# A graph-attention kernel that multiplies by seven products: accumulators in pairs of PSUM banks, emptied by one operation

## The chip, the cores and the metric

The kernel runs on one core of one Trainium2 chip. The metric is the device time of one execution in microseconds (us), the median of several runs. Besides, one execution was recorded by the hardware profiler; its span is counted from the first to the last instruction of the program.

In what follows PE is the matrix engine, PEld its weight load, DVE the vector engine, ACT the scalar engine, POOL the GpSimd engine and SP the engine that issues most DMAs.

## The reference

For each of 32 batch elements x is a 512x512 matrix and adj a 512x512 matrix of zeros and ones. Two graph-attention layers follow each other, the first with four heads of 256 columns, the second with one head of 512:

```python
def gat_layer(x, mask, W, a_src, a_dst, bias, concat):
    xl = (x @ W).reshape(B, N, H, F)
    asrc = jnp.einsum('bnhf,hf->bnh', xl, a_src)
    adst = jnp.einsum('bnhf,hf->bnh', xl, a_dst)
    e = jax.nn.leaky_relu(asrc[:, :, None, :] + adst[:, None, :, :], NEG_SLOPE)
    e = jnp.where(mask[..., None], e, NEG_INF)
    attn = jax.nn.softmax(e, axis=1)
    out = jnp.einsum('bsdh,bshf->bdhf', attn, xl)
    ...
    return out + bias

h = jnp.maximum(_layernorm(x, axis=-1), 0.0)
h = jax.nn.elu(gat_layer(h, mask, W1, att_src1, att_dst1, b1, concat=True))
h = gat_layer(h, mask, W2, att_src2, att_dst2, b2, concat=False)
return x + h
```

All of it is in fp32. Since the softmax sums to one over the sources, adding b2 to each row of the second layer's xl gives the same output as adding b2 to the output.

## The kernel before, in words

Every large product is a 2x2 block product computed with seven block products instead of eight (numbered 1 to 7 in the code). Each of them is a handful of matmuls of a 128x128 stationary block with 256 to 258 moving columns that accumulate in a PSUM bank. The four output blocks are sums of the seven products. Part of these sums is made in PSUM: products 1, 6, 7 and 4 go one after another onto one bank (called a in the code), 5 and 3 onto a second (b), and 2 has a third (g). After each product the bank's present content is read, and the product of the next number accumulates on top of it. So a product on bank a must wait until the content before it has been read.

There are four such stages in a batch element b:

- project1 (line 905): h @ W1, in four units (two row halves of 128 for two pairs of heads), two weight blocks a product, 258 columns (256 and two score columns);
- gather1 (line 1008): attention times xl in layer 1, two units at a time, which are two heads, 256 columns;
- project2 (line 1068): @ W2, two units, four weight blocks a product, 257 columns;
- gather2 (line 1143): attention times xl2 in layer 2, two units, 256 columns.

The matmuls of three of them are laid by `sevens` (line 813), those of gather1 by its own loop. Both take a list that gives the order of (unit, product): TWO, LAST, FOUR, PARTS (lines 840 to 850), PAIRS_OF and, for the last batch element, SINGLY (lines 999 and 1002). For example LAST runs (0,1), (1,1), (0,5), (1,5), (0,6), (1,6), (0,3), (1,3), (0,7), (1,7), (0,2), (1,2), (0,4), (1,4). A bank is one of eight tiles of 512 fp32 columns (line 358), handed out in turn.

What happens after a product is in `put` (line 804) and in gather1: products 1, 4, 5 and 6 are copied by ACT to where the output block lies in SBUF, and 2, 3 and 7 are added to it by DVE:

```python
if n in (1, 4, 5, 6):
    act(COPY, [bk], keys, d, ps, AF.Copy, scale=-1.0)
else:
    dve(ADD, [bk] + keys, keys, nc.vector.tensor_sub, d, d, ps)
```

In gather2 DVE adds each of the seven to a tile that holds x, and there `residual` (line 1103) has loaded x for four row blocks of 128 into four t tiles and has added the bias b2 to each with one DVE operation of 128x512 (line 1114). The t tiles (line 348) serve also as room for the sums t1 and t2 of the right operand in `sums1` (line 956), two for each head. `sums1` makes, for one head, four sums of xl blocks (128x256) and three or four of attention blocks (128x512).

The order of the work is not the order in which the loop at line 1258 states it. Each operation is put on record with its engine, a cost in us, what it reads and writes (lines 378 to 399), and a planner (class Program) lays out the order of each engine. PE's order is that of the program. For ACT, DVE, POOL and SP it takes among the operations that are ready the one with the most urgent rank, and it tries many ranks against its own account of costs. The result is a fixed order for each engine, kept by semaphores at run time. In the program's order the main loop runs gather1 of heads 0 and 1, the first half of project1 of the next batch element, gather1 of heads 2 and 3, the second half of project1, gather2, and project2 of the next element.

In the profile all matmuls bear line 396, all ACT operations line 379, all DVE operations line 382 and most DMAs line 385, as they are issued by helpers. Groups are told apart by tiles: xl<-mm is a copy or sum of project1 or project2, h<-mm or h<-h,mm one of gather1, t<-mm,t one of gather2, t<-t,b_sb the bias.

Of the kernel before, what the change touches and what calls it, by code (L numbers as in the profile page):

```python
# [10 lines left out]
F32 = mybir.dt.float32  # L11
# [19 lines left out]
class Slots:  # L31
# [9 lines left out]
    def give(self, key):  # L41
        self.free.append(key[1])

# [213 lines left out]
def tile_gat(  # L257
# [76 lines left out]
    b2_sb = sbuf.tile([P, DO], F32, name="b2_sb")  # L334
# [8 lines left out]
    adjs = slots("adj", 2, [P, N], I32)  # L343
# [4 lines left out]
    ts_ = slots("t", 4, [P, N])  # L348
# [9 lines left out]
    banks = slots("mm", 8, [P, 512], F32, psum)  # L358
# [42 lines left out]
    COPY, ADD, TINY = 0.28, 0.34, 0.1  # L401

# [54 lines left out]
    def weights2():  # L457

        for (r, c), ix in AT.items():
            dma(  # L460
                1.5, [("ht", 0, 0)], [("w2", ix)], w2_sb[:, ix, :, 1 - c : W2H - c],
# [6 lines left out]
        dma(0.75, (), ["b2"], b2_sb, rows_of(b2, P))  # L468
        for a, v in enumerate((as2, ad2)):
            lk, bc = ts_.take()  # L470
            dma(0.75, (), [lk], bc, rows_of(v[0], P))
            for (r, c), ix in AT.items():
                for k in range(KH):
# [4 lines left out]
                        junk[:, : DO // 2], w2_sb[:, ix, k, 1 - c : W2H - c], 1.0,  # L478
# [5 lines left out]
        for a in range(2):  # L484
            for r in range(2):
                g = part[:, a, r * KH : (r + 1) * KH, :]
                col = slice(0, 1) if a == 0 else slice(W2H - 1, W2H)
# [3 lines left out]
                    w2_sb[:, AT[r, a], :, col], g[:, :, 0:1], g[:, :, 1:2],  # L491
# [308 lines left out]
    def minus(to):  # L800

        def put(n, u, bk, ps):
            d, keys = to(u, *BLOCK[n - 1])
            if n in (1, 4, 5, 6):
                act(COPY, [bk], keys, d, ps, AF.Copy, scale=-1.0)
            else:
                dve(ADD, [bk] + keys, keys, nc.vector.tensor_sub, d, d, ps)

        return put

    def sevens(left, right, rkeys, put, kh, units, width, order):


        bank = {}
        for u, n in order:
            m = units[u][0]
            acc, first = {1: "a", 2: "g", 5: "b", 6: "a", 7: "a", 3: "b", 4: "a"}[n], n in (1, 2, 5)
            if first:  # L820
                bank[u, acc] = banks.take()
            bk, bt = bank[u, acc]
            ps = bt[:, :width]
            a, akeys = left[n]
            pe(
                akeys + rkeys(n), [bk], kh * width / 593,
                [
                    (mm, (ps, a[:, k, m * P : (m + 1) * P], right(n, units[u], k)),
                     dict(start=(first and k == 0), stop=(k == kh - 1), skip_group_check=True))
                    for k in range(kh)  # L830
# [3 lines left out]
            if n in (2, 3, 4):  # L834
                banks.give(bk)
# [517 lines left out]
```

## Time and profile before

| What | us |
|---|---|
| median of 3 runs (lowest to highest) | 2783.35 (2781.97 to 2785.19) |
| span of the profiled execution | 2778.8 |
| DVE, 128x512 bias add, one | 0.689 |
| DVE, 128x258 add from a bank (xl<-xl,mm), one | 0.421 |
| ACT, 128x258 copy from a bank (xl<-mm), one | 0.386 |
| ACT, 128x512 copy from a bank (ht<-mm, eight in the set-up), one | 0.592 |

The profiled execution's span is 4.55 us below the median of the runs; what lies around the span (start and end of the program) is in the run's time and not in the span. A busy share is the time in which at least one instruction of that engine is under way. Matmuls overlap: one takes 0.38 us, and the next begins 0.216 us after it. The durations of ACT and DVE operations overlap at their edges too, so that 372 operations of 0.42 us add up to 149 us of busy time and not to 155.

### The profile page before, as it was taken

Reading aid. Unit: us, or ns where it says so; the run is one execution under the profiler, and the core shown is the slowest. Engines: PE = TensorE matmul, PEld = TensorE weight load, DVE = VectorE, ACT = ScalarE, POOL = GpSimd, SP = SyncE. Lnnn points to the kernel's source line nnn. Section 1 sums busy time; section 2 is a strip of 40 time slices with the busy share of each in tenths; the row PEclk is TensorE's granted clock in tenths of the full one; section 3 lists DMA queues with packets and bytes.
Section 4 is the critical chain, followed back from the end, with each engine's and each line's share of the span. In section 5 each row is a group of like instructions: output and inputs, shape, how many; then the busy total and the mean of one; then the engine's idle time right before and its main releaser. Section 6 shows DMA issues by size and latency. Waiting matters only on the chain. (4 is left out here: it accounts for less than half of the span.)

```text
span 2778.8 us, 41571 instructions
## 1 busy us (share of the span) xinstructions
PE 2746.2 (99%) x12520; PEld 2373.9 (85%) x12520; DVE 2645.4 (95%) x6726; ACT 2304.3 (83%) x4870; POOL 324.7 (12%) x356
## 2 busy tenths in 40 slices
PE   7999999999999999999999999999999999999999
PEld 6688888888888888888888888888888888888887
DVE  7999999999999999999999999999999999998997
ACT  5988888889888888888888888888888888887883
POOL 0110111001111101111011101011110111101110
PEclk9999999999999999999999999999999999999999
DMA  7766767667777667676677766777666867678663
GB/s 228 171 176 178 201 174 199 171 175 181 191 194 174 179 165 203 177 186 184 172 192 184 196 168 175 178 189 195 183 175 175 202 166 202 157 189 182 169 158 107
DMA packets 370964, 501.55 MB, mean 180 GB/s; under 512 B 222260, under 2 KB 226868, under 8 KB 370740
## 3 DMA queue, kind: packets, MB, share of 16 engines
q1 hardware_dynamic: 324948, 332.16, 43.6%
q0 software_dynamic: 45792, 166.74, 25.2%
q8 instruction: 100, 1.64, 0.2%
q14 instruction: 124, 1.02, 0.1%
HBM read 315.89 MB, written 51.31 MB: 132 GB/s over the span
## 5 line engine op out<-in xcount | busy, mean ns | idle before, releaser
L396 PE MATMUL mm<-w_sb,hs 128*128 128x257 f32 (+2 forms) x3032 | 688.5, 381 | 4.9 <-DVE hs L382 2.5
L396 PEld LDWEIGHTS mm<-w_sb,hs 128*128 128x128 f32 x3032 | 575.8, 190 | 92.0 <-ACT xl L379 4.6
L390 POOL DMA_DIRECT2D p<-dm x314 | 276.2, 887 | 2346.3 <-DVE p L382 1600.3
L379 ACT ACTIVATE l<-as,z 128x512 f32<-128x512 f32 x640 | 442.8, 721 | 101.9 <-DMA as<-das 96.2
L379 ACT ACTIVATE l<-l,low 128x512 f32<-128x512 f32 x640 | 459.2, 721 | 49.1 <-DVE low L382 46.0
L396 PE MATMUL mm<-w_sb,ht 128*128 128x258 f32 x2112 | 481.4, 382 | 1.9 <-DVE xl L382 1.4
L396 PE MATMUL mm<-p,xl 128*128 128x256 f32 (+1 forms) x1984 | 468.0, 384 | 1.0 <-DVE h L382 0.8
L396 PE MATMUL mm<-w_sb,h 128*128 128x257 f32 x2056 | 467.8, 379 | 0.0
L379 ACT ACTIVATE p<-p,z 128x512 f32<-128x512 f32 (+1 forms) x636 | 427.2, 716 | 42.6 <-DMA p<-dm 28.1
L382 DVE SCALAR_TENSOR_TENSOR p<-rr,z 128x512 f32<-128x512 f32 (+1 forms) x636 | 449.0, 743 | 11.8 <-DMA rr<-drr 11.6
L396 PEld LDWEIGHTS mm<-w_sb,ht 128*128 128x128 f32 x2112 | 400.9, 190 | 61.8 <-DVE xl L382 4.1
L382 DVE CUSTOM_DVE_ANT_1 l<-l,mt 128x512 f32<-128x512 f32 x640 | 429.1, 685 | 12.0 <-ACT l L379 9.5
L396 PEld LDWEIGHTS mm<-w_sb,h 128*128 128x128 f32 x2056 | 389.4, 189 | 57.8 <-issue 0.5
L396 PEld LDWEIGHTS mm<-p,xl 128*128 128x128 f32 x1984 | 377.1, 190 | 61.7 <-issue 5.7
L379 ACT ACTIVATE xl<-mm 128x258 f32<-128x258 f32 (+2 forms) x748 | 279.8, 382 | 70.6 <-PE mm L396 68.7
L379 ACT ACTIVATE h<-mm 128x256 f32<-128x256 f32 x496 | 181.7, 378 | 91.0 <-PE mm L396 88.4
L382 DVE TENSOR_TENSOR xl<-xl,mm 128x258 f32<-128x258 f32 x558 | 222.8, 420 | 29.1 <-PE mm L396 24.3
L379 ACT ACTIVATE xr<-h,b_sb 128x512 f32<-128x512 f32 x248 | 176.7, 721 | 75.7 <-DVE h L382 72.0
L396 PE MATMUL mm<-t,hs 128*128 128x256 f32 x992 | 226.0, 380 | 2.9 <-ACT h L379 2.9
L396 PEld LDWEIGHTS mm<-t,hs 128*128 128x128 f32 x992 | 188.4, 190 | 29.9 <-ACT h L379 4.7
L382 DVE SCALAR_TENSOR_TENSOR h<-h,b_sb,xr 128x512 f32<-128x512 f32 x248 | 182.9, 747 | 3.2 <-ACT xr L379 3.1
L382 DVE TENSOR_TENSOR t<-mm,t 128x256 f32<-128x256 f32 (+1 forms) x424 | 172.8, 419 | 11.7 <-PE mm L396 10.5
(114 smaller groups left out, 3421.8 us busy)
## 6 DMA issues: line engine op xcount, KB each, us to landing
p<-dm POOLq DMA_DIRECT2D x314, 512.0 KB, 5.2
rr<-drr SPq DMA_DIRECT2D x159, 512.0 KB
x<-in_x_dram SPq DMA_DIRECT2D x129, 256.0 KB
adj<-in_adj_dram SPq DMA_DIRECT2D x128, 256.0 KB
as<-das SPq DMA_DIRECT2D x64, 512.0 KB
t<-in_x_dram SPq DMA_DIRECT2D x124, 256.0 KB
out_dram<-t SPq DMA_DIRECT2D x124, 256.0 KB
dm<-m SPq DMA_DIRECT2D x32, 512.0 KB
```

Of the source, the lines that this page charges most:

```text
L379: prog.add("ACT", cost, reads, writes, lambda: nc.scalar.activation(*a, **k))
L382: prog.add("DVE", cost, reads, writes, lambda: f(*a, **k))
L390: lambda: nc.gpsimd.dma_start(to, at, accum_op=OP.add), size,
L396: f(*a, **k)
```

## The change

The eight single banks become four tiles of two banks each, handed out by a new class. `take2` gives a whole pair, `take` one half. For each bank it keeps how many columns have been written by matmuls since the last fresh start, and a bank that is to be filled by ACT and then accumulated upon is chosen only where that width is enough. Among the fitting pairs the least written is taken.

```diff
+    def able(self, seeded):
+        return any(
+            all(q in self.free and self.written[q] >= seeded for q in ((i, 0), (i, 1)))
+            for i in range(len(self.tiles))
+        )
+    def take2(self, width, seeded=0):
+        whole = [i for i, j in self.free if j == 0 and (i, 1) in self.free]
+        least = {i: min(self.written[i, j] for j in range(2)) for i in whole}
+        i = min((i for i in whole if least[i] >= seeded), key=least.get)
...
+        return [("mm", i, j) for j in range(2)], self.tiles[i]
-    ts_ = slots("t", 4, [P, N])
+    ts_ = slots("t", 2, [P, 2, N])
-    banks = slots("mm", 8, [P, 512], F32, psum)
+    banks = Banks(tiles("mm", 4, [P, 2, 512], F32, psum))
+    COPY2, ADD2 = 0.5, 0.61
```

In `sevens` two units form one step: both products go into the two banks of a pair, and one ACT or DVE operation of twice the width empties both. After product 1 the pair is copied by ACT into a second pair, g, if one is free, and not to the output; product 2 then accumulates on that copy, and g is copied to the output by ACT. So DVE adds product 2 only where there was no pair for the copy. Two of the order lists fall away, and a seed can be laid into a fresh pair before its first product:

```diff
+            acc, first = ACC[n], n in (1, 5) or n == 2 and us not in forked
             if first:
+                seed = seeds.get(n)
+                bank[us, acc] = banks.take2(width, 0 if seed is None else M)
+                if seed is not None:
+                    first = False
+                    bks, bt = bank[us, acc]
+                    act(
+                        COPY2, [seed[1]], bks, bt[:, :, :width],
+                        seed[0][:, None, :].to_broadcast([P, 2, width]), AF.Copy,
+                    )
...
+            if n == 1 and banks.able(width):
+                bank[us, "g"] = gks, gt = banks.take2(width, width)
+                act(COPY2, bks, gks, gt[:, :, :width], bt[:, :, :width], AF.Copy)
+                forked.add(us)
+            else:
+                fresh = n in (1, 4, 5, 6) or n == 2 and us in forked
+                put(n, [units[u] for u in us], bks, bt[:, :, :width], fresh)
...
+    LAST = tuple(((0, 1), n) for n in (1, 5, 6, 3, 7, 2, 4))
+    FOUR = LAST + tuple(((2, 3), n) for _, n in LAST)
+    PARTS = tuple(((0, 1), n) for n in (1, 2, 5, 6, 3, 7, 4))
```

gather1 does the same with two heads as a step (in SINGLY one head, one bank), with the copy of product 1 always made. Its `sums1` makes the four sums of xl for both heads in one operation each, and takes one paired t tile a head, given back when products 5 and 6 are both through:

```diff
-        tuple((h + i, n) for n in (1, 2, 6, 5, 7, 3, 4) for i in range(2)) for h in (0, 2)
+    PAIRS_OF = tuple(tuple(((h, h + 1), n) for n in (1, 5, 6, 2, 7, 3, 4)) for h in (0, 2))
...
-            if n in (1, 4, 5, 6):
-                act(COPY, [bk], [key], to, ps, AF.Copy)
+            if n == 1:
+                bank[u, "g"] = gks, gt = some(len(u), M)
+                act(COPY2 if two else COPY, bks, gks, gt[:, :, :M], ps, AF.Copy)
+            elif n in (2, 4, 5, 6):
+                act(COPY2 if two else COPY, bks, keys, to, ps, AF.Copy)
             else:
-                dve(ADD, [bk, key], [key], nc.vector.tensor_add, to, to, ps)
+                dve(ADD2 if two else ADD, bks + keys, keys, nc.vector.tensor_add, to, to, ps)
```

The bias b2 no longer goes onto x. project2 lays it, with its sign turned, into the pairs of products 1 and 5, and so into the rows of xl2; for this the set-up holds b2 as two halves, the second less the first. Each half of xl2 and of W2 now has its 256 columns first and the score column last. `residual` loads two row blocks with one DMA and adds nothing, and gather2 writes two row blocks out with one:

```diff
+            {1: (b2_sb[:, 0], "b2"), 5: (b2_sb[:, 1], "b2")},
...
-            dma(0.75, [x2_key(b, 0, 0)], halves, xr, x[b, d * P : (d + 1) * P, :])
-            dve(0.59, [xk, "b2"], halves, nc.vector.tensor_add, xr, xr, b2_sb)
+            dma(
+                1.5, [x2_key(b, 0, 0)], halves, xr,
+                x[b, r * 2 * P : (r + 1) * 2 * P, :].rearrange("(m p) f -> p m f", p=P),
+            )
```

Costs and orders that the planner sees change with this, so the orders of ACT, DVE, POOL and SP are laid anew over the whole kernel.

## The prediction

> **What bounds the kernel now.** I read the page's first part, then the windows by stage, then the timeline of PE, then the waits of PE, and last the groups by form for the instructions that the change replaces.
>
> ```profile
> span 2778.8 us, 41571 instructions
> PE 2746.2 (99%) x12520; PEld 2373.9 (85%) x12520; DVE 2645.4 (95%) x6726; ACT 2304.3 (83%) x4870; POOL 324.7 (12%) x356
> ```
> ```profile
> 176.00:2505.00 2329.00, 2323.82 (x10703) 2029.28 (x10702) 2249.94 (x5660) 1982.20 (x4185) 278.28 (x301) 1.00 0.70 182
> 2505.00:2700.00 195.00, 189.22 (x857) 162.87 (x856) 182.47 (x454) 159.92 (x343) 24.21 (x27) 0.99 0.73 175
> 2700.00:2778.80 78.80, 73.86 (x308) 57.50 (x306) 57.84 (x136) 32.74 (x70) 1.73 (x2) 0.99 0.34 104
> ```
>
> The columns after each window's length are busy time of PE, PEld, DVE, ACT and POOL, then clock and DMA share. In the 2329 us of the main loop PE idles 5.2 us. It idles 5.8 us in the next stretch, 4.9 us in the last, and by subtraction 16.7 us in the first 176 us, of which 11.5 us pass before the first matmul. That is all the idle time there is.
>
> A busy PE could still be slow, so I look at the pace:
>
> ```profile
> 300.77 3.61 PE L396 MATMUL mm<-p,xl 128*128 128x256 f32 x16
> 304.22 3.62 PE L396 MATMUL mm<-t,hs 128*128 128x256 f32 x16
> 307.68 1.89 PE L396 MATMUL mm<-p,xl 128*128 128x256 f32 x8
> ```
>
> 16 matmuls from start to start take 3.46 us, 0.216 us each. 12,520 of them would take 2704 us; the 257, 258 and 512 columns wide ones bring the sum to about 2730. The pace is steady, so time can come only out of gaps, and the waits of PE name those:
>
> ```profile
> PE mm L396 <- ACT x L379: 11.8, 2, 11.5
> PE mm L396 <- DVE hs L382: 3.9, 4, 2.2
> PE mm L396 <- ACT h L379: 3.1, 5, 1.6
> PE mm L396 <- ACT xl L379: 2.4, 4, 1.0
> PE mm L396 <- ACT w_sb L379: 2.2, 1, 2.2
> PE mm L396 <- ACT p L379: 1.7, 2, 1.2
> PE mm L396 <- DVE h L382: 1.5, 2, 0.8
> PE mm L396 <- DVE xl L382: 1.4, 3, 0.9
> ```
>
> Apart from the first wait they are twenty-odd short stalls, 16 us together. The change keeps every product, so it can win only part of these; it can lose without such a limit.
>
> **What the Trainium skill says.** "Perfetto Trace Analysis", Optimizing Scalar/DVE Operations, gives each ACT or DVE instruction a fixed access overhead, and says that larger operations help if the engine is saturated, and that breaking them up lets work finish sooner where they cause bubbles elsewhere. Both halves bear on this case. The trace agrees with the first: a 128x256 add from PSUM takes 0.42 us, a 128x512 one 0.69. "PSUM — Partial Sum Buffer", Rule 2 under The four PSUM rules, says that ACT's writes leave the has_written bits alone, and that a matmul without the first flag adds where the bit is set. That is why the new bank list keeps a written width. No run here shows it yet. "ScalarE: Activation LUTs", Step-by-step, says that ACT writes PSUM sooner than SBUF; the trace before has no ACT write to PSUM.
>
> **The change, part by part.** The rows:
>
> ```profile
> L379 ACT ACTIVATE h<-mm 128x256 f32<-128x256 f32 x496 | 181.7, 378 | 91.0 <-PE mm L396 88.4 <-DVE p L382 0.5
> L382 DVE TENSOR_TENSOR h<-h,mm 128x256 f32<-128x256 f32 x372 | 149.5, 417 | 13.5 <-PE mm L396 11.0 <-ACT h L379 0.6
> L382 DVE TENSOR_TENSOR t<-t,b_sb 128x512 f32<-128x512 f32 x124 | 82.0, 689 | 2.4 <-DMA t<-in_x_dram 2.3
> L382 DVE TENSOR_TENSOR t<-mm,t 128x512 f32<-128x512 f32 x4 | 2.8, 690 | 5.5 <-PE mm L396 5.5
> ```
>
> *DVE.* The other rows that go, in busy time: xl<-xl,mm 148.9 (258 wide, x372) and 73.9 us (257 wide, x186), t<-mm,t 170.1 us (x420), the four hs/xl sums of 256 columns 202.4 us (x496). With 149.5 and the bias adds' 82.0 this makes 826.8 us. In their place come pair operations at 0.69 us (the last row above). Product 2 is no longer added by DVE in layer 1 and the projections, and product 1 in gather2 is copied instead. So 248/2 + 248/2 + 124/2 + 360/2 + 496/2 = 738 operations, 509 us. DVE loses 318 us: from 2645 to about 2327, 84% of the span.
>
> *ACT.* What goes: 186.8 + 181.7 + 91.5 = 460 us of 256 to 258 wide copies. What comes: five pair copies per group (product 1 into the second bank, then 5, 6, 2, 4) for 62 groups of project1 and as many of gather1, five in each of 31 project2 passes and two bias seeds in 32, and one in each of 31 gather2 passes: 870. The nearest row is ht<-mm 128x512, 592 ns (busy 0.56 each), so 487 to 515 us: ACT gains 27 to 55 us and ends near 84%. A copy from PSUM to PSUM is not in the trace; by the page it could be a little shorter, and I take the row.
>
> None of this time lies on the path while PE is busy. What it does is give DVE room.
>
> *Hand-over of a bank.* This part lies on the path. Before, the two banks of a pair of units were emptied apart, and between a product and the next one on the same bank lay three other products (for instance in LAST: (0,1), then (1,1), (0,5), (1,5), then (0,6)). Now one operation waits for both units, and only one pair, two products, lies between (1, 5, 6: bank a again). With two weight blocks a product is four matmuls, 0.865 us. A modelled matmul end lies 0.38 us after its start and the next start 0.216 us after it, so before the bank was due 3 x 0.865 - 0.16 = 2.43 us after its product ended, now 2 x 0.865 - 0.16 = 1.57. Of it go up to 0.14 us until the reader starts (a t<-mm,t of the main loop), the reader (0.38, now 0.59 on ACT; 0.42, now 0.69 on DVE), and 0.05 us until PE starts. The slack falls from about 1.85 us to 0.79 (ACT) and 0.69 (DVE). An ACT engine in the middle of something longer than that makes PE wait. ACT's long ones are ht<-x, 1358 ns, adj<-x, 1048 ns (four each per batch element), and the exponential with its accumulator read, 721 + 198 ns (twenty).
>
> Price: per 86.5 us (one batch element) a random arrival meets an ht<-x with more than 0.79 us to run in 4 x 0.57 / 86.5 = 2.6% of cases and then waits 0.28 us longer on average; with adj<-x and the exponential this makes 0.011 us per hand-over. I count 15 ACT hand-overs with one pair between in a batch element (four in each of two project1 groups, three in each of two gather1 groups, one in gather2), so 0.16 us, 5 us over 31. On DVE (12 of them: two in each of those four groups, four in gather2; the long ones are the four 1.22 us sums of h) the same sum gives 3 us. Both engines run a written order made by a planner that knows these durations and that can place the copies, so I take 5 of these 8 us. Bounds: 0, if it places all of them; and 40, if half of the 27 hand-overs stand behind one more operation and are 0.1 us late (27 x 31 x 0.5 x 0.1).
>
> *Copy of product 1 to a second bank.* In gather1, project1 and gather2 product 2 now needs that copy, but two or more pairs later, so it costs only ACT time. In the last element's SINGLY order one product lies between: 0.70 us are there and 0.57 are needed. Four places, up to 0.3 us each: 1 us. By the bookkeeping of the list the copy is made in every group except the last project2, and the new groups live on three of the four pairs, because the list prefers the least written one. So product 1 of project1 often takes the pair that the gather's product 3 has just left, one pair earlier. These are among the 12 on DVE.
>
> *Bias.* The 124 adds go (counted). The seeds wait for an earlier group's pair and stand before products 1 and 5 of project2, whose pair of products lasts twice as long (3.46 us): no cost. The set-up grows by one memset, two small operations and a smaller load, beside the first project1: under 1 us.
>
> *DMA.* x and out move in 62 issues each of 512 KB in place of 124 of 256 KB; SP has fewer issues, and the first put of gather2 is a group away from the load. t tiles come as two pairs in place of four singles, given back after product 6 in place of one after 5, one after 6: nothing waits on them at that place. Cost 0, bounds -1 and +3.
>
> *What DVE's room gives back.* Of the 5.2 us of stalls in the main loop, and some 0.1 us of refilling at each of a dozen, I let 4 us go; of 10.7 us after 2505 us, where p, h and w_sb are late, 5 us; of the first 176 us, 3 us. That is 12 us; 0 and 20 are the ends.
>
> Sum: -12 + 5 + 1 = -6 us on the profiled 2778.8, so a span near 2773. The median of the runs, 2783.35, lies 4.55 us above the span; I keep that: 2777.
>
> **Rivals.**
> 1. *The room finds no taker* (no change). PE's stalls come from chains (DMA, p, the planner's misses) and not from DVE's load, or the new hand-overs eat the gain: 2783. For: DVE at 95% lets PE run for hundreds of us without a gap. Against: the hs, h and xl waits stand on DVE itself.
> 2. *The hand-over becomes the bound* (slower). Place: project1 and gather1, products 1, 5, 6 on bank a. Price: 0.05 us on each of 837 hand-overs is 42 us; less the 12 won, plus 1, 2814. At 0.013 us on average the two sides cancel, and from 0.02 us on the loss can be told. For: slack is less than half, and ACT stands in its own order behind waits such as l <- DMA as<-das (96.2 us in 36). Against: ACT waits for PE, not the other way round, in h<-mm (88.4 us), so it is often early, and many of the as waits lie in gather2, which has one ACT copy.
> 3. *Full recovery* (faster by more): the planner, with DVE and ACT both at 84%, closes nearly every gap after the start-up: -18, 2765.
>
> **How the numbers follow.** A measurement of this kernel can tell about 0.2%, 5.6 us, from no change. Chances: my forecast with rival 3 (which has 0.08 of it) 0.50, rival 1 0.18, rival 2 0.32. The forecast's own range is 2764 to 2782. For eight in ten I need the lower two thirds of rival 2, so 2764 to 2802.
>
> **What will show it.** Right: DVE near 84%, ACT near 84%, PE waits on DVE hs and xl gone, at most 5 us of new waits on ACT h, ACT xl and the copies into mm. Wrong: PE waiting for mm copies or for DVE adds in every batch element, or PE busy growing at the same count of matmuls. The size is wrong if the recovered stalls reappear behind p or a DMA.

## The result and the profile after

The changed kernel takes 2860.36 us (median of 4 runs, 2858.08 to 2862.4) against 2782.66 us for the kernel before in the same series: a ratio of 1.0275, 95% interval 1.0249 to 1.0301. The forecast was 2777 us, with 2802 at the upper end of its range. The profiled execution's span is 2856.3 us, 77.5 us longer than before. First the head of its page, then its windows by stage (length, then busy time of PE, PEld, DVE, ACT and POOL with instruction counts, clock, DMA share, GB/s):

```profile
span 2856.3 us, 39591 instructions
PE 2770.0 (97%) x12520; PEld 2373.9 (83%) x12520; DVE 2432.2 (85%) x5494; ACT 2384.9 (83%) x4506; POOL 322.6 (11%) x356
```
```profile
0.00:176.00 176.00, 151.90 (x618) 117.02 (x619) 145.42 (x438) 124.40 (x242) 18.82 (x26) 0.98 0.71 187
176.00:2505.00 2329.00, 2284.89 (x10436) 1978.41 (x10435) 2006.72 (x4446) 2001.83 (x3762) 269.63 (x293) 0.99 0.70 178
2505.00:2700.00 195.00, 194.02 (x893) 168.82 (x893) 173.80 (x380) 172.17 (x321) 23.75 (x26) 1.00 0.67 179
2700.00:2856.30 156.30, 139.21 (x578) 109.61 (x576) 106.29 (x233) 86.50 (x184) 10.38 (x12) 0.97 0.43 122
```

The 77.5 us have three parts. In the main loop PE idles 44.1 us where it idled 5.2: 38.9 more. In the three other stretches together it idles 42.2 us where it idled 27.4: 14.8 more. And PE's busy time itself has grown from 2746.2 to 2770.0 at the same 12,520 matmuls: 23.8 more. The waits of PE, in the same columns as before, say on whom:

```profile
PE mm L439 <- ACT mm L422: 24.1, 17, 5.4
PE mm L439 <- ACT h L422: 19.7, 12, 5.6
PE mm L439 <- ACT x L422: 11.8, 1, 11.8
PE mm L439 <- DVE hs L425: 5.6, 3, 4.1
PE mm L439 <- DVE t L425: 5.1, 6, 1.2
PE mm L439 <- DVE w_sb L425: 3.3, 1, 3.3
```

The first, for the copy of product 1 into a second bank (mm), is new, and the second, for the emptying of gather1's banks (h), has grown from 3.1 us: together 29 waits with 43.8 us, single ones over 5 us. A pair that is emptied a little late in every batch element would look different: many short waits. So the question is what ACT itself waits for. Its waits for DMA, before and after (total, times, longest):

```profile
ACT l L379 <- DMA as<-das: 96.2, 36, 6.3
ACT p L379 <- DMA p<-dm: 28.1, 27, 3.6
ACT ht L379 <- DMA x<-adj: 5.9, 6, 1.5
```
```profile
ACT p L422 <- DMA p<-dm: 51.2, 31, 9.8
ACT l L422 <- DMA as<-das: 30.7, 24, 5.1
ACT ht L422 <- DMA x<-adj: 30.2, 9, 8.2
ACT adj L422 <- DMA x<-adj: 6.9, 2, 5.5
```

Two kinds of transfer are waited for longer: p<-dm, by which POOL's queue adds the mask to p (an accumulation, in what follows), and x<-adj, by which SP transposes the normalised x. It is not that more is moved: the DMA share of the main loop is 0.70 before and after. One stop shows how PE comes to wait. The timeline of the changed kernel (start, length, engine, instruction, and in brackets the idle time before it), POOL and SP's queue first, then ACT, then PE:

```profile
1699.80 0.86 POOL L433 DMA_DIRECT2D p<-dm  x1 [0.46 <-PE mm L439]
...
1699.83 5.22 SPq L637 DMA_TRANSPOSE x<-adj  x2
...
1714.71 1.33 ACT L422 ACTIVATE p<-p,z 128x512 f32<-128x512 f32 x2 [6.88 <-DMA p<-dm]
1715.95 0.58 ACT L422 ACTIVATE xl<-mm 128x514 f32<-128x514 f32 x1
1716.42 0.80 ACT L422 ACTIVATE x<-x,stats 128x512 f32<-128x512 f32 x1
1717.13 1.04 ACT L422 ACTIVATE adj<-x 128x1024 uint16<-128x1024 uint16 x1
1718.08 0.58 ACT L422 ACTIVATE mm<-mm 128x512 f32<-128x512 f32 x1
...
1711.40 1.89 PE L439 MATMUL mm<-t,hs 128*128 128x256 f32 x8
1718.71 1.65 PE L439 MATMUL mm<-t,hs 128*128 128x256 f32 x3 [5.42 <-ACT mm L422]
```

The accumulation and the first of two transposes were issued 0.03 us apart. The exponential that needs the accumulation starts 14.9 us later, where this kernel's median from issue to landing is 5.6 us. ACT takes its work in a written order, so it stands for 6.88 us; behind the two exponentials come three more operations, and only then the bank copy that PE's next product needs. PE loses 5.42 us. None of these operations is slow; one transfer is.

The other stops are of the same kind. Take each wait of PE in the main loop back to the engine that ended it, and look for that engine's longest standstill in the 8 us before: of 43.9 us in 34 waits, 19.0 us lie behind a stand of ACT for x<-adj and 18.0 us behind one for p<-dm. In the kernel before the two together make 0.6 us.

A long stop can cost twice. The windows of the changed kernel around this one, 3.4 us just after the stop and the 10.5 us after those, and 3.4 us at the end of another stop, of 3.68 us:

```profile
1718.70:1722.10 3.40, 3.39 (x9) 2.74 (x10) 2.38 (x4) 2.66 (x3) 0.86 (x1) 0.54 0.80 154
1722.50:1733.00 10.50, 10.50 (x50) 9.22 (x49) 9.39 (x15) 9.36 (x14) 1.72 (x2) 1.00 0.99 261
242.00:245.40 3.40, 3.22 (x15) 2.79 (x16) 3.40 (x6) 3.40 (x7) 0.86 (x1) 1.00 0.75 242
```

The clock (the figure after the busy times) is 0.54 in the first and 1.00 in the second, and PE begins 9 matmuls in 3.4 us where the usual pace of 0.216 us makes 15. In the third it stays 1.00: not every stop draws a lower clock. Over the whole trace the mean clock is 0.993 of 2856.3 us, against 0.998 of 2778.8 us before, so by this estimate some 15 us of the 23.8 us by which PE's busy time has grown come from the clock. Some 6 us more, again an estimate, follow from the overlap of matmuls: the last one before a wait has no follower that begins after 0.216 of its 0.38 us, which adds 0.16 us of busy time each, and there are 61 waits where there were 25.

From the trace's semaphore events one can work out when each transpose of x landed. Over 8 us after its issue landed 5 of 120 before and 25 of 120 after.

### The profile page after: what moved, and what is told of

Read it like the earlier page. It is cut to its first block, busy times and chain, and to the rows that moved or that the text cites. A ratio compares the mean times of both kernels' runs of the same rounds, so it can differ in the third digit from the quotient of the medians.

```text
span 2856.3 us, 39591 instructions
## 1 busy us (share of the span) xinstructions
PE 2770.0 (97%) x12520; PEld 2373.9 (83%) x12520; DVE 2432.2 (85%) x5494; ACT 2384.9 (83%) x4506; POOL 322.6 (11%) x356
## 3 DMA queue, kind: packets, MB, share of 16 engines
q0 software_dynamic: 45792, 166.74, 25.6%
## 4 chain that ended last, share of the span: by engine, by line
PE 79%; DMA 9%; ACT 5%; DVE 5%; issue 2%; SPq 0%; POOL 0%; ACTq 0%; POOLq 0%; DVEq 0%
PE mm L439 79%; DMA p<-dm 4%; DMA x<-adj 3%; DVE p L425 1%; ACT l L422 1%; ACT p L422 1%; DMA as<-das 1%; ACT adj L422 1%; ACT ht L422 1%; DVE l L425 1%; DVE t L425 1%; DVE hs L425 1%; DVE h L425 1%; ACT xl L422 0%; ACT xr L422 0%
## 5 line engine op out<-in xcount | busy, mean ns | idle before, releaser
L439 PE MATMUL mm<-w_sb,hs 128*128 128x257 f32 (+2 forms) x3032 | 685.3, 383 | 25.1 <-ACT h L422 16.1
L422 ACT ACTIVATE l<-l,low 128x512 f32<-128x512 f32 x640 | 455.2, 713 | 40.0 <-DVE low L425 39.3
L422 ACT ACTIVATE p<-p,z 128x512 f32<-128x512 f32 (+1 forms) x636 | 424.7, 709 | 62.3 <-DMA p<-dm 51.2
L422 ACT ACTIVATE l<-as,z 128x512 f32<-128x512 f32 x640 | 436.9, 712 | 32.0 <-DMA as<-das 30.7
L439 PE MATMUL mm<-w_sb,h 128*128 128x257 f32 x2056 | 459.5, 380 | 3.3 <-DVE w_sb L425 3.3
L425 DVE SCALAR_TENSOR_TENSOR p<-rr,z 128x512 f32<-128x512 f32 (+1 forms) x636 | 448.1, 740 | 15.8 <-DMA rr<-drr 15.1
L422 ACT ACTIVATE xl<-mm 128x516 f32<-128x516 f32 (+2 forms) x376 | 218.4, 586 | 46.9 <-PE mm L439 45.6
L439 PE MATMUL mm<-t,hs 128*128 128x256 f32 x992 | 233.1, 386 | 25.0 <-ACT mm L422 22.0
L439 PEld LDWEIGHTS mm<-t,hs 128*128 128x128 f32 x992 | 189.7, 193 | 57.5 <-ACT mm L422 27.1
L425 DVE SCALAR_TENSOR_TENSOR h<-h,b_sb,xr 128x512 f32<-128x512 f32 x248 | 181.5, 744 | 46.5 <-ACT xr L422 46.4
L422 ACT ACTIVATE ht<-x 128x1024 uint16<-128x1024 uint16 x120 | 159.3, 1351 | 30.2 <-DMA x<-adj 30.2
L439 PE MATMUL mm<-xl,p 128*128 128x256 f32 (+1 forms) x752 | 180.2, 388 | 2.3 <-DVE t L425 1.6
L422 ACT ACTIVATE h<-mm 128x512 f32<-128x512 f32 (+1 forms) x256 | 146.3, 574 | 26.5 <-PE mm L439 24.4
```

The source lines that it names most:

```text
L422: prog.add("ACT", cost, reads, writes, lambda: nc.scalar.activation(*a, **k))
L425: prog.add("DVE", cost, reads, writes, lambda: f(*a, **k))
L439: f(*a, **k)
```

## The experiments

Three theories. The **collision**: transposes and accumulations that are under way together land late, ACT stands in its order before what needs them, and emptyings of banks are queued behind. The **hand-over** (rival 2 of the prediction): a pair emptied by one operation leaves too little slack, whatever the DMAs do. The **shared pair**: single banks that lie in one pair make PE wait for each other's reader; this can act only where single banks are used, at the two ends. Some expectations shorten these to C, H and T; CH says that late transfers and short slack are both needed. Since every edit but the leaving out of a transfer makes the planner lay a new order, two runs with nothing changed but its costs show how far orders scatter.

All runs in one table; "before" was 2782.7 to 2790.3 us in the series concerned, and the ratio is against that. "Late" counts transposes that landed over 8 us after issue; "ACT" is its waits for p<-dm and x<-adj; "main" and "ends" are PE's idle time from 176 to 2505 us and outside, all in us. These four columns are of the one profiled execution, which can lie some way from the median (2876.6 us for a_ap6, 2881.8 for a_htdve).

| Run | Median | Ratio [95%] | Late | ACT | Main | Ends |
|---|---|---|---|---|---|---|
| before | 2782.7 | | 5 | 34 | 5.2 | 27.4 |
| after | 2860.4 | 1.0275 [1.0249, 1.0301] | 25 | 88 | 44.1 | 42.2 |
| b_noise | 2793.7 | 1.0036 [1.0023, 1.0049] | 5 | 35 | 15.8 | 25.6 |
| a_noise | 2853.6 | 1.0247 [1.0215, 1.0280] | 18 | 83 | 39.3 | 41.4 |
| b_apart | 2785.8 | 0.9997 [0.9980, 1.0013] | 12 | 32 | 9.5 | 26.1 |
| a_apart | 2826.8 | 1.0157 [1.0123, 1.0190] | 24 | 47 | 18.3 | 40.8 |
| b_ap6 | 2832.4 | 1.0195 [1.0158, 1.0232] | 8 | 43 | 27.6 | 33.6 |
| a_ap6 | 2856.8 | 1.0274 [1.0230, 1.0318] | 26 | 88 | 53.8 | 46.5 |
| a_split_ap6 | 2941.8 | 1.0566 [1.0545, 1.0586] | 13 | 33 | 56.6 | 68.8 |
| a_tiles_ap6 | 2856.7 | 1.0257 [1.0225, 1.0289] | 25 | 78 | 40.3 | 43.0 |
| b_nodm | 2766.2 | 0.9918 [0.9888, 0.9947] | 0 | 0 | 2.5 | 22.8 |
| a_nodm | 2791.5 | 1.0010 [0.9997, 1.0023] | 0 | 2 | 3.5 | 37.8 |
| b_nott | 2772.3 | 0.9937 [0.9918, 0.9957] | none | 28 | 3.6 | 23.7 |
| a_nott | 2802.0 | 1.0053 [1.0038, 1.0069] | none | 33 | 8.1 | 39.2 |
| a_ends_nodm | 2782.2 | 0.9981 [0.9969, 0.9992] | 0 | 0 | 4.4 | 31.8 |
| a_nobias | 2818.3 | 1.0123 [1.0101, 1.0146] | 16 | 48 | 22.3 | 43.6 |
| a_nofork | 2843.1 | 1.0215 [1.0192, 1.0239] | 13 | 80 | 27.1 | 44.3 |
| a_htdve | 2869.2 | 1.0303 [1.0270, 1.0336] | 24 | 61 | 58.2 | 44.2 |
| a_dvemask | 2807.9 | 1.0087 [1.0071, 1.0103] | 0 | 41 | 10.9 | 34.9 |
| a_all | 2841.9 | 1.0207 [1.0190, 1.0225] | 22 | 37 | 37.1 | 37.1 |

**How far orders scatter.** Names with a_ are edits of the changed kernel, with b_ of the kernel before.

```diff
-    COPY2, ADD2 = 0.5, 0.61
+    COPY2, ADD2 = 0.51, 0.62
```

> The changed kernel with the planner's costs of a pair copy and pair add raised by 0.01 us: all orders laid anew, 23 planned collisions as against 24. Theory C and theory H both: 2835 to 2885, so that the loss belongs to the kind of order and not to one unlucky one. If it falls under 2820, a new order alone moves the time by as much as the change did, and single undoings can't be read without their traces.

> The kernel before with the planner's costs of a bank copy and add raised by 0.005 us, so that all orders are laid anew; by the planner's own account 25 transposes have a p<-dm issued within 1.5 us after them, in place of 17, as many as in the changed kernel (24). Theory C in its plain form (late DMA alone is enough): 10 to 25 slow transposes, and 2800 to 2850 although the banks are emptied singly. Theory CH (collision and short slack are both needed): the slow transposes come, but PE idles under 20 us in the main loop, and the time is 2780 to 2800. If the time stays within 5 us of the kernel before and slow transposes do not come, the account of collisions doesn't foretell them.

Orders of the same work lie some 10 us apart (2853.6 against 2860.4, 2793.7 against 2784.1), and of the 77 us some 60 or more stay. By this one redraw of each, the loss is not one unlucky order. The run b_noise was also a test, and the collision's forecast missed: 25 transposes were planned with an accumulation within 1.5 us after them, as many as in the changed kernel (24), yet only 5 landed late. So nearness in the plan does not foretell a late transfer. And as the late transfers did not come, the test of CH that this run was meant to be did not take place.

**Planned apart.** The planner issues no accumulation for 2.5 us after a transpose of x, and nothing from SP for 1.0 us after an accumulation; in the ap6 runs 6.0 and 3.0 us.

```diff
+            if jobs[j][0] == "SP" and jobs[j][4] == 1.27:
+                self.apart["POOL"] = t + 2.5
+            if jobs[j][0] == "POOL" and jobs[j][4] is not None:
+                self.apart["SP"] = t + 1.0
...
+                t = max(t, hold, self.apart.get(e, 0.0))
```

> The changed kernel with one rule more for the planner: after an x transpose by DMA is issued on SP, POOL issues no accumulating DMA (p<-dm) for 2.5 us, and SP issues nothing for 1.0 us after a p<-dm. Nothing else is changed. Theory C (collision): the transposes that take over 8 us (25 of 120 in the changed kernel, 5 of 120 before) do so because a p<-dm is issued within about 1.5 us of them; ACT, which works in a fixed order, then stands before an operation that needs the late data, and the bank copies behind it are late. Then slow transposes fall to 5 or fewer, PE's idle time in 176 to 2505 us falls from 44 to under 15 us, PE's granted clock rises to 0.997, and the time to 2790 to 2815. Theory H (hand-over): the slack of each bank hand-over is too short whatever DMA does; the time stays at 2845 to 2865.

> The kernel before with the same rule. Theory C: it has few collisions to lose, so it gains little: 2765 to 2782. Theory H says nothing else; if it gains as much as the changed kernel does from the rule, the rule helps by something other than what the change brought.

> The changed kernel with the planner's spacing rule widened: POOL issues no p<-dm for 6.0 us after an x transpose, SP nothing for 3.0 us after a p<-dm. With 2.5 and 1.0 us in the plan (a_apart) the engines' drift at run time was enough to bring them within 1.3 us again: 24 transposes still took over 8 us. Theory C: now slow transposes fall to 5 or fewer, ACT's waits for x<-adj and p<-dm from 42 us (a_apart) to under 25, PE's idle time in 176 to 2505 us under 12 us, and the time goes to 2795 to 2815. Theory H (short slack at each hand-over is the loss by itself): PE's idle time in the main loop stays at 15 us or more though the slow transposes are gone, and the time stays at 2815 to 2835.

> The kernel before with the same wide rule. Theory C: 2775 to 2790 (its collisions were few), 5 or fewer slow transposes. A gain of over 10 us would say that the rule helps any order.

The narrow rule gains 34 us on the changed kernel and nothing on the one before. That is the side the collision wants, but not its size (at most 2815 us), and 24 transposes still land late where 5 were expected: the rule holds in the plan only. In the trace of a_apart 50 of 120 transposes have an accumulation issued within 1.5 us before or after them, in that of the changed kernel 42. What went down is ACT's standing (88 to 47 us). The wide rule missed too: 26 transposes are late, the changed kernel stays where it was (2856.8 us), and the kernel before loses 48 us. A plan that no longer fits what happens may be the reason; no run shows it. So these four were no clean test of the collision.

**Each bank emptied by its own operation**, the pairs otherwise kept, and single banks in another first order, both with the wide rule:

```diff
-                act(COPY2, bks, keys, d, ps, AF.Copy, scale=-1.0)
+                act(COPY, [bks[i]], k, d[:, i], ps[:, i], AF.Copy, scale=-1.0)
...
-        self.free = [(i, j) for i in range(len(tiles)) for j in range(2)]
+        self.free = [(i, j) for j in range(2) for i in range(len(tiles))]
```

> The changed kernel with the wide rule, and each bank emptied by an operation of its own again (two copies or adds of 256 to 258 columns in place of one of 512 to 516); pairs, copy of product 1, seeds, loads and stores stay. The slack of a hand-over is again that of the kernel before (1.85 us), at the price of some 50 us more of ACT and DVE time each. Theory H: PE's waits on ACT mm, ACT h and ACT xl fall by more than half against a_ap6 and the time is 10 us or more below it. Theory C: within 8 us of a_ap6, either way.

> The changed kernel with the wide rule, and the list of free banks in another order, so that two single banks taken one after another lie in different tiles. Theory T: the single-bank stretches at both ends (0 to 176 us and after 2700 us) lost time because two banks of one tile are kept apart as if they were one: the second product of a head waits until the first one's bank has been read (the three PE waits of 1.15 us on xr<-mm in the first 110 us, two on t<-mm,t in the last 20). Then these five waits vanish and the time is 4 to 10 us below a_ap6. Otherwise within 3 us of it.

Single emptying against a_ap6 costs 85 us more, with many short waits (26 on DVE's t, 22 on ACT's h), where the hand-over theory expected a gain of 10 us and the collision a change within 8. The form "the double-width operation is the loss" gets no support. But operations are added here and all orders are new, so the run does not refute the hand-over by itself. It also shows that PE can lose as much time with ACT's waits for the two transfers no longer than before (33 us). The other list order changes nothing (2856.7 against 2856.8); it reaches only the banks' first use, since pairs come back side by side.

**One of the two transfers left out**, with the written order kept to the instruction. This is the clean test. In nodm POOL's accumulations are not issued, and the exponential that follows them is a scaled copy of the same size; in nott the transposes are not issued, and ACT's copy ht<-x takes x untransposed. The lines below are those of nodm; nott puts `lambda: None` in the place of the transpose.

```diff
-            lambda: nc.gpsimd.dma_start(to, at, accum_op=OP.add), size,
+            lambda: None, size,
```

> The changed kernel with its written order untouched, but the mask is not added to p by a DMA (the accumulating transfers p <- dm are left out, and the exponential after them is a plain scaled copy of the same size). Theory of the collision (transposes of x and these transfers that are issued together land late, and ACT stands before an operation that needs them, with bank copies queued behind): the transposes x <- adj over 8 us fall from 25 to at most 8, the ACT waits p <- dm (51 us) are gone, PE's idle time in the main loop falls from 44 us to 15 or less, and the time is at most 25 us above that of the kernel before with the same left out. Theory of the hand-over (a bank pair that is emptied later, whatever the DMAs do): PE's idle time in the main loop stays above 30 us and the difference to before stays at 50 us or more.

> The kernel before with the same left out (no p <- dm, a scaled copy in place of the exponential). Theory of the collision: little to win, since PE lost only 5 us in the main loop: 2770 to 2784 us. Theory of the hand-over: the same.

> The changed kernel with its written order untouched, but the DMA transposes x <- adj are left out (ht gets x untransposed, by a copy of the same size); the accumulating transfers stay. Theory of the collision: p <- dm lands earlier, ACT's waits for it fall from 51 us to about the 28 of before, PE's idle time in the main loop falls to 20 us or less, and the time is at most 30 us above the kernel before with the same left out. A rival within it, that p <- dm is late because DVE hands p over earlier in a bunch and not because of the transposes: ACT's waits for p <- dm stay at 45 us or more. Theory of the hand-over: the difference to before stays at 50 us or more.

> The kernel before with the transposes x <- adj left out in the same way. All theories: 2765 to 2784 us; ACT's waits for p <- dm stay near 28 us.

Without the accumulations no transpose takes over 7.1 us, in either kernel, and the difference between the kernels shrinks from 77.7 to 25.3 us (at most 25 were expected). Without the transposes it shrinks to 29.7 us (at most 30). The two kernels of each of these differences ran in one series; between that series and the first the kernel before itself differs by 7.6 us, so the shrinking is known no better than that. The kernel before gains a little more than expected, too: 2766.2 us where 2770 was the lower end. The main loop of the changed and of the earlier kernel without accumulations, then PE's waits in the changed one:

```profile
176.00:2505.00 2329.00, 2325.49 (x10710) 2028.30 (x10709) 2061.06 (x4566) 2009.77 (x3859) 38.90 (x28) 1.00 0.42 121
```
```profile
176.00:2505.00 2329.00, 2326.49 (x10728) 2033.62 (x10727) 2257.24 (x5678) 1947.56 (x4195) 37.34 (x28) 1.00 0.44 122
```
```profile
PE mm L439 <- DVE hs L425: 5.8, 4, 4.0
PE mm L439 <- DVE t L425: 5.2, 6, 1.3
...
PE mm L439 <- ACT mm L422: 1.5, 3, 0.5
...
PE mm L439 <- ACT h L422: 0.9, 2, 0.5
```

PE idles 3.5 us in the changed main loop and 2.5 in the other. The waits for mm and h, 43.8 us, are down to 2.4. With all its pairs, copies and seeds in the same order, the changed main loop runs as tightly as the old one, so the hand-over by itself is not what loses the time. Whether its shorter slack is needed besides, so that the same late transfers would have cost the kernel before less, no run shows. And the two transfers are late because of each other: with the transposes gone ACT's waits for the accumulations, still there, fall from 51.2 to

```profile
ACT p L422 <- DMA p<-dm: 32.8, 20, 9.8
```

while in the kernel before the same step leaves them where they were (28.1 to 28.4). The landings say the same. In all 18 traces with transposes, each that took over 8 us had an accumulation under way at the same time, and none without one took over 7.1 us. What the collision explains is thus some 50 us of the 77.

**The other 25 us.** Between a_nodm and b_nodm the spans differ by 25.9 us: PE idles 1.0 us more in the main loop, 15.0 more at the ends, and is busy 9.9 more. The theory of the shared pair was put to a run in which a single bank is never taken from the pair of the one before:

```diff
+        half = next((q for q in fit if q[0] != self.last), half)
+        self.last = half[0]
         self.free.remove(half)
```

> The changed kernel with the mask's accumulating transfers left out as in the run before of that kind (2791.5 us, 25 us above the kernel before with the same left out), and with single banks handed out so that two in a row never lie in the same pair. Theory of the ends (what is left of the loss without the colliding transfers is PE waiting, at the start and the end, for the reader of the other bank of the same pair): the waits xr <- mm (2.3 us) and t <- mm,t (5.2 us) fall to under 2 us together, and the time to 2780 to 2787 us. Rival (those waits are the length of one eviction and lie in the order of the work): no difference of more than 3 us.

It gains 9.3 us (8.8 us between the two profiled spans; the series differ by 5 us in the kernel before). PE's waits for DVE's t fall from 5.2 us to

```profile
PE mm L442 <- DVE t L428: 1.6, 2, 0.8
```

and the waits for ACT's xr (2.3 us in 3) are no longer in the list. So some 9 us of the loss come from the stretches at the start and the end that work with single banks (gather1_plain, SINGLY and gather2_plain in the code) and take both halves of a pair in a row. Part of the gain may be the new order of the start (PE's wait on hs fell from 5.8 to 3.5 us). The last 16 us of difference to b_nodm stay open; the waits on hs, w_sb and between the banks of PARTS are part of them.

**One part of the change undone.** Without the seeds (DVE adds the bias to x, two operations for a pair of row blocks), and without the copy of product 1 (product 2 has a fresh bank, DVE adds it, order 1, 2, 6, 5, 7, 3, 4):

```diff
-            {1: (b2_sb[:, 0], "b2"), 5: (b2_sb[:, 1], "b2")},
...
-            if n == 1 and banks.able(width):
+            if False:
```

> The changed kernel without the bias in the banks: project2 begins with an empty bank again, and DVE adds the bias to the residual by two operations of 128 x 512 for each pair of row blocks. ACT loses some 35 us, DVE gains some 80 us. Theory of the collision: the transposes that land late stay in number (15 or more over 8 us), PE's idle time in the main loop 25 us or more, time 2815 to 2865 us. Rival (the two seeds in ACT's order are what PE waits for): 2800 us or less.

> The changed kernel without the copy of product 1 to a second bank: product 2 has a fresh bank, DVE adds it, and the seven products come in the order 1, 2, 6, 5, 7, 3, 4. ACT loses some 90 us, DVE gains some 115 us. Theory of the copies (a queue on ACT in which the bank copy stands behind a late transfer is needed for the loss, and this copy is the main one): PE's wait for mm <- mm on ACT is gone, and the time is 2800 us or less. Theory of the collision alone: another emptying takes the copy's place behind the late transfers; 15 or more transposes over 8 us, PE's idle time in the main loop 30 us or more, time 2820 us or more.

Neither cures it: 16 and 13 transposes stay late, and without the copy PE waits for other emptyings in ACT's order (h 17.3 us in 10, xl 8.1 in 9; what is left on mm, 5.1 us, are the seeds). The theory that the copy itself is needed for the loss falls. The collision's own bounds were set a little high: 22.3 and 27.1 us of idle time in the main loop where 25 and 30 were expected, 13 late transposes where 15 were. Both gain, 42 and 17 us, and both give DVE work back: DVE is busy 2501.7 and 2532.7 us against 2432.2. That fits a DVE with less room, but each is also a new order, so it isn't shown to be the reason.

**The waiting copy moved to DVE:**

```diff
-            act(
-                1.21, [xk], [("ht", t, 0), ("ht", t, 1)],
+            dve(
+                1.21, [xk], [("ht", t, 0), ("ht", t, 1)], nc.vector.tensor_copy,
```

> The changed kernel with the copy ht <- x, which waits for the transpose, put on DVE in place of ACT (116 copies; ACT loses some 155 us, DVE gains as much or less). Theory of the queue: a late transpose no longer stops ACT; ACT's waits for x <- adj are gone and PE's waits for ACT's mm <- mm and h fall by half or more, but DVE now waits for the transposes and with it its adds from the banks; the waits of ACT for p <- dm stay. Time 2815 to 2850 us. Rival (the transposes set PE back through ht itself): no gain, 2850 us or more.

This is 9 us slower still by the medians, though the two intervals overlap; it is the rival's number (2850 us or more). The wait moves with the copy, and grows:

```profile
DVE ht L425 <- DMA x<-adj: 69.8, 23, 6.5
```
```profile
L425 DVE COPY ht<-x 128x1024 uint16<-128x1024 uint16 x120 | 88.8, 741 | 69.9 <-DMA x<-adj 69.8
```

PE now waits for DVE's h (16.1 us in 7) and for hs, which is made from ht (15.7 in 6), as well as for ACT's mm (28.4 in 12). The expected gain did not come: two engines with written orders stand before late transfers in place of one (ACT's 61 us in the table are now nearly all accumulations), though the copy itself is quicker there (741 ns against ACT's 1351).

**Looking for a version that is faster than both.** First the mask of heads 0 and 1 added by DVE, which takes 120 of 318 accumulations away, with the narrow rule and the single banks apart; then the narrow rule, no seeds and single banks apart together.

```diff
-            here = self.layer == 2 and self.b == B - 1
+            here = self.layer == 2 and self.b == B - 1 or self.layer == 1 and 0 < self.b < B - 1 and h in (0, 1)
```

> A version meant to be faster than both: the changed kernel with DVE's new room spent on the mask of heads 0 and 1 of the first layer (eight adds p <- p,m of 128 x 512 for each batch element, some 165 us of DVE, in place of 120 of the 318 accumulating transfers), with no transfer of x by transpose planned within 2.5 us before an accumulation nor within 1.0 us after it, and with single banks in a row from different pairs. Theory of the collision: 10 or fewer transposes over 8 us, PE's idle time in the main loop under 15 us, time 2770 to 2800 us. If it is DVE's load that PE then waits for: DVE at 93%, PE's waits on DVE's h, t and xl above 15 us, time 2800 us or more.

> The changed kernel without the bias in the banks, with transposes and accumulations planned apart (2.5 and 1.0 us) and single banks in a row from different pairs: three edits that gained 42, 34 and 9 us apart, of which the first two meet the same loss. Theory of the collision: they do not add up; 2780 to 2810 us, 8 to 18 transposes over 8 us, PE's idle time in the main loop 8 to 20 us. If they did add up: 2775 us.

With fewer accumulations no transpose is late, though all pairs are kept, and the main loop has 10.9 us of idle time:

```profile
176.00:2505.00 2329.00, 2318.14 (x10644) 2012.38 (x10643) 2157.82 (x4751) 2040.56 (x3836) 204.29 (x189) 1.00 0.57 157
```

At 2807.9 us it gains 52 us on the changed kernel and misses the expected range by 8; DVE, at 91% busy, is waited for with 6.1 us only, so its load is not the reason. It is the fastest of the changed kernels that compute everything, and still 0.9% slower than the one before. a_all missed its range by 32 us: 22 transposes are late, and gains of single edits (42, 34 and 9 us) don't carry over once the order is laid anew. Its loss is also of another kind. ACT's waits for the two transfers are hardly longer than before (37 us), but it stands for as<-das and for DVE's row minima (low):

```profile
ACT l L431 <- DVE low L434: 114.2, 51, 5.0
ACT l L431 <- DMA as<-das: 55.8, 38, 6.2
```

Of the 36.9 us of PE's waits in its main loop, 21.4 lie behind these two stands and 12.9 behind those for x<-adj and p<-dm. So it is ACT's standing in its written order that makes PE wait, and late transfers are one way to it. No version that computes everything beat the kernel before.

## Why the prediction was wrong

*What bounds the kernel, and the ceiling of a gain* held. The statement that the change "can lose without such a limit" held too.

*DVE and ACT.* The rows were priced well: the seven new kinds of pair operation on DVE take 682 to 691 ns (0.69 was taken), ACT's 580 to 600 (592). Their sum gives DVE the 318 us less that were forecast. But the engine's busy time fell by 213 us only, from 2645.4 to 2432.2, and ACT's rose by 81, not by 27 to 55. A row's busy time still contains its overlap with its neighbours of other rows: before, all DVE rows add up to 3104.5 us for 2645.4 us of busy engine, after to 2761.4 for 2432.2. That fewer instructions overlap less is a reading of these sums. The term was too large by 105 us, without consequence for the time. The new rows, as the groups by form show them:

```profile
L422 ACT ACTIVATE mm<-mm 128x512 f32<-128x512 f32 x91 | 53.2, 584 | 4.6 <-PE mm L439 4.0
L422 ACT ACTIVATE mm<-b_sb 128x514 f32<-128x514 f32 x64 | 38.0, 594 | 35.1 <-DVE t L425 35.0
...
L425 DVE TENSOR_TENSOR h<-h,mm 128x512 f32<-128x512 f32 x120 | 81.8, 682 | 20.8 <-PE mm L439 20.2
```

*Copy from bank to bank.* The page "ScalarE: Activation LUTs" of the Trainium skill, Step-by-step, has ACT write PSUM sooner than SBUF. Here 584 ns for mm<-mm stand beside 586 for h<-mm of the same size: no difference, and taking the row was right. That ACT's writes leave the written bits alone ("PSUM — Partial Sum Buffer", Rule 2) agrees with these runs: products 2, 1 and 5 accumulate on copied or seeded banks in every batch element.

*Hand-over* (5 us, at most 40). This is one of the two terms that failed. It took what can stand in front of a bank's reader to be ACT's own long instructions, at random, 0.3 us late. Those cost next to nothing: a_nodm has the same hand-overs and loses 2.4 us on mm and h. What stood in front was an operation waiting 2 to 8 us for a transfer, with the emptying up to five places behind it. Rival 2 named the place ("ACT stands in its own order behind waits") but with as<-das, which became cheaper (96.2 to 30.7 us), and with 0.05 us each time; its 2814 was the right side with the wrong price. In a_all as<-das does count.

*DMA* ("Cost 0, bounds -1 and +3"). This is the other. The sum counted the loads of x and the stores of the output, the transfers that the diff edits. It left out those that only move in time. Counted from the first matmul of each project2, accumulations issued after 8 to 12 us fall from 58 to 34 and those after 12 to 16 us rise from 32 to 52, just when the first transposes go out; those after 24 to 28 us fall from 18 to 7. Transposes with two accumulations issued within 1 us before to 2 us after them rise from 1 to 14, but that alone does not make them late: b_noise has 8, at a median of 5.4 us, and a_all has none with 22 late. A price for the two kinds of transfer meeting, by the runs: 50 us.

*What DVE's room gives back* (-12 us). It gave nothing. PE's waits on DVE's hs rose from 3.9 to 5.6 us, on its t and w_sb from 0.2 to 8.4. The room was priced as a gain alone; that it also lets p be ready at other times, and with it starts transfers, had no term. That the room is why the accumulations bunch is not shown: a_nobias and a_nofork, which give DVE work back, still have 60 and 47 of them after 12 to 16 us. Also open is why a transpose with an accumulation issued between 0.5 us before it and 1.5 us after it takes a median 9.0 us in the changed kernel and 5.6 in the one before, though there are nearly as many such (29 and 25).

*Clock.* No term. PE's busy time grew by 23.8 us, some 15 us of it by the clock after stops. The list of what would show the prediction wrong had it ("PE busy growing at the same count of matmuls").

*The rest.* The set-up's cost stayed small. The ends were forecast to gain 8 us and lost 14.8; single banks in pairs, some 9 us with what follows, were not seen. The 4.55 us kept between span and median are too many: around the span itself the runs show 1.8 us (2858.08 against 2856.3), the rest is scatter between executions.

## What to carry to other kernels

A change that relieves an engine and lays the orders anew also moves the times at which transfers start: before pricing room as gain, list every DMA whose start hangs on that engine and what else is under way then. In a kernel with written orders, the slack of a hand-over is to be compared with the longest wait of an operation ahead of it in the same queue, not with that operation's length. Leaving one transfer out while the order stays is the experiment that tells a late transfer from a tight hand-over, once it is done to both kernels; here a rule in the plan didn't, because the execution did not keep to it.

## What the runs showed of the hardware

- Transposes of x (128x1024 of 2 bytes, 256 KB) take a median 3.2 us and at most 7.1 from issue to landing when no accumulating transfer is about (b_nodm and a_nodm), and up to 14.9 us beside 512 KB accumulations (after). Those take a median of 5.2 us and at most 9.4 where no transpose is under way with them, 6.5 and at most 15.2 where one is (after); a longer transfer meets a transpose more easily, so these medians alone prove little.
- After PE stood still for 5.42 us its clock was 0.54 for 3.4 us, and then whole again; after another stop, of 3.68 us, it stayed 1.00 (after).
- A strided 2-byte copy of 128x1024 (ht<-x) takes 741 ns on DVE (a_htdve) and 1351 ns on ACT (after).
- A copy of 128x512 from PSUM takes ACT 584 ns into PSUM and 586 ns into SBUF (after).
